# Zeroing a gather table: the whole table, or its border cells alone

## The chip, the cores and the metric

The kernel runs on one core of a Trainium2 chip. The metric is the device time of one launch in microseconds. Five engines matter: PE (TensorE, matmuls), DVE (VectorE), ACT (ScalarE), POOL (GpSimd) and SP (SyncE, which here only issues transfers). Each works through its own list of instructions in order. Transfers between HBM and on-chip memory (SBUF) run on 16 DMA engines that all queues share. In this kernel SP feeds the queue that the profile calls q1 (hardware_dynamic), and POOL feeds q0 (software_dynamic).

## The reference, cut to what matters

The input is an image batch `x` of shape (2, 64, 64, 128). Four layers follow each other, each adding to `x`: layer 0 is a convolution with a selective scan in four directions; layer 1 is a deformable 3x3 convolution; layer 2 is a second scan model and a spectral convolution; layer 3 is a linear attention and a mixture of experts. Each needs the whole output of the one before.

The change is in layer 1. For each output pixel and each of 9 taps a learned offset gives a fractional position; the four pixels around it are gathered, weighted and summed, and a pixel outside the image counts as zero:

```python
def gather(yi, xi):
    valid = (yi >= 0) & (yi < H) & (xi >= 0) & (xi < W)
    yc = jnp.clip(yi, 0, H - 1)
    xc = jnp.clip(xi, 0, W - 1)
    v = x[b_idx, yc, xc]
    return v * valid[..., None].astype(x.dtype)
val = gather(y0i, x0i) * ((1 - wy) * (1 - wx))[..., None] + gather(y0i, x0i + 1) * ((1 - wy) * wx)[..., None] + gather(y0i + 1, x0i) * (wy * (1 - wx))[..., None] + gather(y0i + 1, x0i + 1) * (wy * wx)[..., None]
out = jnp.einsum('bhwkc,kcf->bhwf', val, kernel.reshape(KK, C, F))
```

## The kernel before, in words

**The table.** Layer 1 gathers from a table in HBM. For each image it has 67 x 67 cells (`TS` = 67), and a cell holds the four neighbouring pixels of one position side by side: 4 quadrants of C = 128 floats, 2,048 bytes. Both images make 2 x 67 x 67 x 2,048 bytes = 18.39 MB. Positions are clamped so that every gather lands inside the table (lines 498 to 503), and a quadrant that lies outside the image must read as zero. Layer 1 writes the image into the table with 16 transfers on SP's queue (line 462). Quadrant (dy, dx) is written to rows 2-dy to 65-dy and columns 2-dx to 65-dx. So the cells in rows 2 to 64 and columns 2 to 64 get all four quadrants from the image, and rows and columns 0, 1, 65 and 66 keep zeros in some quadrant or in all.

**Where the zeros come from.** `zero_table` (line 412) runs at the very beginning, before layer 0. It sets a tile `z` of 128 x 536 floats to zero with POOL and sends it over the whole table with one transfer on POOL's queue: 8,576 pieces of 2,144 bytes. The tile is in a pool of its own (`zt`, line 1355) that is given back at once, so that the first tiles of layer 0 lie in the same memory: `w_xp` (line 169), `w_dt`, `sel` (line 174), `w_out`, `mean_w` (line 180), `an` and `dd`. Their first writers have to wait until the zero transfer has read `z` to the end. These writers are SP's loads of `w_xp`, `w_dt` and `w_out`, DVE's memset of `sel`, and ACT's exponential that makes `an` (line 183).

**What goes on at the same time.** SP loads two vectors of parameters (`pv`, `rv`), then the image `X` in eight transfers of 512 KB (`move`, line 1333; layer 0's first image is the first four), then the 64 KB matrix `gmat` (line 200) and `w_in`. [...] Layer 0 then begins with image 0: PE transposes `X` (line 95), DVE gathers statistics (`groupnorm`, line 126: lines 132 to 146), PE averages them over channel groups with `gmat` (lines 136 and 143), DVE makes the inverse root (`rsqrt`, lines 81 to 87) and normalises `xt` (line 146). With that PE computes `pz` (line 209) and `px` (line 221), then the depthwise convolution as 288 matmuls `pc` (line 227). Only then does the scan loop start (lines 241 to 376).

**Order.** The code is written with a tile framework. The list of each engine is ordered when the program is built, by a scheduler that has its own idea of how long a transfer takes, and waits are put in where memory is reused. So instructions that stand at one place in the source can be issued earlier or later than their line says.

Of the kernel before, what the change touches and what calls it, by code (L numbers as in the profile page):

```python
# [16 lines left out]
F32 = mybir.dt.float32  # L17
# [8 lines left out]
P = 128  # L26
B, HH, WW, C = 2, 64, 64, 128
# [13 lines left out]
TS = 67  # L41
# [369 lines left out]

def zero_table(k, pool, table):

    nc = k.nc
    row = B * TS * 4
    z = pool.tile([P, row], F32, name="zero")
    nc.gpsimd.memset(z, 0.0)
    flat = table.rearrange("a c -> (a c)").rearrange("(p g f) -> p g f", p=P, f=row)
    nc.gpsimd.dma_start(out=flat, in_=z.unsqueeze(1).to_broadcast([P, TS, row]))


def layer1(k, table):
# [915 lines left out]
def kernel(tc, ins, out, stages=STAGES):  # L1338
    nc = tc.nc
    with ExitStack() as es:  # L1340
# [8 lines left out]
        if two or "0" in stages or "1" in stages:  # L1349
            with tc.tile_pool(name="x01", bufs=1) as xp:  # L1350
                k.X = xp.tile([P, NT, C], F32, name="X")
                move(nc, k.X, tokens(x))
                if "1" in stages:
                    table = dr.tile([B * TS * TS, 4 * C], F32, name="table")
                    with tc.tile_pool(name="zt", bufs=1) as zp:
                        zero_table(k, zp, table)
                if "0" in stages:
                    layer0(k)
                with ExitStack() as e2:
                    if two:  # L1360
                        mix = mixing_weights(k, dr, e2)
                    if "1" in stages:
                        layer1(k, table)
                    if two:
                        weights = mix()
                if two:
                    norm_tokens(k, rs, sh)
                x = dr.tile([B * L, C], F32, name="x1")
                move(nc, tokens(x), k.X)
# [119 lines left out]
```

## Time and profile before

| | us |
|---|---|
| median of 3 runs | 16227.84 |
| lowest and highest | 16219.87 and 16235.26 |
| the profiled execution, its time | 16221.3 |
| its span, first to last instruction | 16219.5 |
| busy in the span: DVE | 13938.5 |
| POOL | 13438.3 |
| PE | 12269.0 |
| ACT | 9683.1 |

The span is the profiled execution from its first instruction to its last; 1.8 us lie around it. Its time lies 6.5 us below the median of the runs. Busy times of engines overlap and don't add up to the span.

A view by time windows gives, for each stretch, the busy time of each engine with its number of instructions, the TensorE clock that was granted (PEclk, 1.00 is full speed), the busy share of the DMA engines and what they moved. A view of waits says for how long an engine sat idle before a group of instructions and what ended that. A view of transfers gives, by queue, packets, megabytes, and the time that these packets took as a share of 16 engines over the window. The timeline gives start and length in us.

### The profile page before, as it was taken

The numbers are of one execution on the slowest core, as the hardware profiler recorded it, in microseconds if no ns is written. First come the engines' busy times: TensorE is split into PE (matmuls) and PEld (weight loads), VectorE is DVE, ScalarE is ACT, GpSimd is POOL, SyncE is SP. The second block draws the span as 40 slices with busy tenths as digits, with TensorE's granted clock in tenths as the row PEclk, the third lists the DMA queues.
The fourth block names the chain that finished last, engine by engine and source line by source line (L and its number), as shares of the span: only waits on it lengthen the run. The fifth ranks groups of instructions, "written<-read, shape, count | busy, mean of one in ns | idle before, by whom it ended". The sixth has DMA issues, their size and how long they took to land.

```text
span 16219.5 us, 191958 instructions
## 1 busy us (share of the span) xinstructions
PE 12269.0 (76%) x69886; PEld 7241.8 (45%) x69886; DVE 13938.5 (86%) x13011; ACT 9683.1 (60%) x15720; POOL 13438.3 (83%) x4181
## 2 busy tenths in 40 slices
PE   6666657666657874548688688888888888888897
PEld 2222223222225861215455355555545555555565
DVE  4999985999974349999999999999999999999973
ACT  3555534555520017777777677777777777777752
POOL 3888744888735879999999999999999999999970
PEclk8999989999988886769899799999999999999998
DMA  2111111111125544546565555655666666665553
GB/s 101 68 68 66 66 48 52 68 68 66 66 73 162 161 146 151 164 153 198 180 195 193 171 187 192 195 190 196 189 199 195 192 204 196 188 205 195 187 173 128
DMA packets 1214866, 2389.74 MB, mean 147 GB/s; under 512 B 346648, under 2 KB 923288, under 8 KB 1047904
## 3 DMA queue, kind: packets, MB, share of 16 engines
q1 hardware_dynamic: 1162672, 2206.74, 41.5%
q0 software_dynamic: 50384, 169.42, 3.5%
q8 instruction: 552, 9.04, 0.2%
q14 instruction: 394, 3.23, 0.1%
q10 hardware_dynamic: 864, 1.32, 0.0%
HBM read 2018.49 MB, written 358.65 MB: 147 GB/s over the span
## 4 chain that ended last, share of the span: by engine, by line
POOL 39%; DVE 18%; PE 15%; issue 5%; ACT 3%; DMA 3%; another core or an unknown queue 1%; SPq 0%; POOLq 0%; DVEq 0%; ACTq 0%
POOL S L1064 33%; DVE S L1120 11%; PE pef L948 6%; DVE S L347 5%; POOL G L516 2%; PE Z L1082 2%; DMA row<-drow 2%; PE acc L921 2%; POOL S L342 2%; PE pv L535 1%; PE pw L747 1%; PE po L468 1%; POOL S L1070 1%; DVE M L361 1%
## 5 line engine op out<-in xcount | busy, mean ns | idle before, releaser
L1120 DVE TENSOR_TENSOR_SCAN S<-dA,S 128x512 f32<-128x512 f32 x8192 | 9225.0, 1200 | 391.1 <-ACT dA L1118 209.4
L1064 POOL TENSOR_TENSOR S<-row,g 128x4096 f32<-128x4096 f32 x1024 | 9102.1, 8896 | 251.8 <-DMA row<-drow 191.1
L1118 ACT ACTIVATE dA<-row,a_t 128x512 f32<-128x512 f32 x8192 | 5615.4, 692 | 2148.0 <-DVE S L1120 2111.3
L1082 PE MATMUL Z<-S,cv 128*32 128x256 f32 x32768 | 2503.1, 435 | 1481.5 <-ACT ze L1088 1225.6
L948 PE MATMUL pef<-hk,ur 128*128 128x256 f32 x14336 | 3515.4, 388 | 135.4 <-ACT e L928 119.9
L948 PEld LDWEIGHTS pef<-hk,ur 128*128 128x128 f32 x14336 | 2647.1, 191 | 1076.7 <-issue 565.5
L342 POOL TENSOR_TENSOR S<-du,br 128x1024 f32<-128x1024 f32 x1024 | 2389.7, 2355 | 204.8 <-issue 109.2
L347 DVE TENSOR_TENSOR_SCAN S<-dA,stt,S 128x512 f32<-128x512 f32 x1792 | 2198.3, 1268 | 127.7 <-POOL S L342 95.5
L1082 PEld LDWEIGHTS Z<-S,cv 128*32 128x32 f32 x32768 | 1000.8, 121 | 2690.6 <-issue 1283.4
L376 PE MATMUL yp<-M,ident 128*128 128x512 f32 x4096 | 2091.7, 635 | 3.2 <-DVE M L361 3.2
L376 PEld LDWEIGHTS yp<-M,ident 128*128 128x128 f32 x4096 | 821.5, 201 | 2180.2 <-issue 2141.7
L345 ACT ACTIVATE dA<-dt,an 128x512 f32<-128x512 f32 x2048 | 1332.3, 680 | 187.5 <-DVE S L347 173.3
L316 PE MATMUL pcn<-cs,sel 80*128 80x512 bf16 x1024 | 405.6, 396 | 1261.6 <-DVE M L361 1212.4
L361 DVE TENSOR_TENSOR M<-S,pcn 128x1024 f32<-128x1024 f32 x1024 | 1250.6, 1221 | 108.2 <-PE pcn L316 4.8
L1088 ACT COPY ze<-Z 128x512 f32<-128x512 f32 x1024 | 1122.9, 1097 | 234.1 <-PE Z L1082 200.2
L921 PE MATMUL acc<-e,mw 128*128 128x512 f32 x1920 | 1043.5, 631 | 31.7 <-ACT e L928 31.1
L516 POOL DMA_INDIRECT G<-table,idx x576 | 797.1, 1384 | 261.1 <-issue 175.1
L349 ACT COPY stt<-S 128x2 f32<-128x2 f32 x896 | 170.8, 191 | 1376.3 <-DVE S L347 1365.7
L948 PEld LDWEIGHTS pef<-hd,ur 128*128 128x128 f32 x4096 | 758.1, 194 | 493.9 <-issue 235.4
L948 PE MATMUL pef<-hd,ur 128*128 128x256 f32 (+1 forms) x4096 | 876.7, 340 | 103.2 <-ACT e L928 97.2
L523 DVE TENSOR_TENSOR V<-G,wt 128x4608 f32<-128x4608 f32 x64 | 317.6, 4962 | 603.3 <-DMA G<-table,idx 594.8
L279 POOL TENSOR_TENSOR r<-xd,cs 80x512 f32<-80x512 f32 x64 | 73.8, 1152 | 798.2 <-ACT cs L265 798.2
(319 smaller groups left out, 9010.1 us busy)
## 6 DMA issues: line engine op xcount, KB each, us to landing
row<-drow SPq DMA_DIRECT2D x1024, 1024.0 KB
br<-bc SPq DMA_DIRECT2D x256, 1024.0 KB
zd<-ze SPq DMA_DIRECT2D x1024, 256.0 KB
hk<-in_phi_dram SPq DMA_DIRECT2D x128, 576.5 KB
hk<-in_phi_dram SPq DMA_DIRECT2D x96, 704.5 KB
hd<-in_phi_dram SPq DMA_DIRECT2D x512, 128.5 KB
mw<-wdr SPq DMA_DIRECT2D x480, 128.0 KB
hk<-in_phi_dram SPq DMA_DIRECT2D x160, 320.5 KB
```

Of the source, the lines that this page charges most:

```text
L342: nc.gpsimd.tensor_tensor(S, du, br[:, n % 4, :].unsqueeze(1).to_broadcast([P, 2, T]), ALU.mult)
L345: nc.scalar.activation(dA, dt[:, h, :], AF.Exp, scale=an[:, kk * 2 + h, n : n + 1])
L347: nc.vector.tensor_tensor_scan(S[:, h, s_], dA[:, s_], S[:, h, s_], init, ALU.mult, ALU.add)
L361: nc.vector.tensor_tensor(M, S, pcn.unsqueeze(1).to_broadcast([P, 2, T]), ALU.mult)
L376: nc.tensor.matmul(yp[:, h, :], k.ident, M[:, h, :], start=False, stop=n == 15)
L921: nc.tensor.matmul(acc.rearrange("p a s -> p (a s)"), ms[f][:, o, :], e, start=box["first"], stop="whole" in box and (f, o) == todo[-1])
L948: nc.tensor.matmul(pe[:, a, 256 - n :], ur[:, par, j, :], h[:, at : at + n], start=i == 0, stop=i + 1 == len(mm))
L1064: nc.gpsimd.tensor_tensor(S, row.unsqueeze(1).to_broadcast([P, 2, R, T]), g.unsqueeze(2).to_broadcast([P, 2, R, T]), ALU.mult)
L1082: nc.tensor.matmul(Z[32 * j : 32 * j + 32, q], cv[:, h, s], S[:, h, :, s], start=h == 0, stop=h == 1)
L1088: nc.scalar.copy(ze.rearrange("p q t e -> p q e t"), Z)
L1118: nc.scalar.activation(dA, row[:, j % R, :], AF.Exp, scale=a_t[:, h, d : d + 1])
L1120: nc.vector.tensor_tensor_scan(s, dA, s, 0.0, ALU.mult, ALU.add)
```

## The change: what it does

`zero_table` no longer fills the whole table. For each of the two images it sends two transfers of 128 x 536 floats (rows 0 and 1, rows 65 and 66, 274 KB each) and one of 64 x 2,048 floats (524 KB): 64 runs of four cells, each the last two cells of a row and the first two of the next. That is 2.15 MB in six transfers, all on POOL's queue. The tile `z` becomes 128 x 2,048 floats.

```diff
 def zero_table(k, pool, table):
 
+
     nc = k.nc
-    row = B * TS * 4
-    z = pool.tile([P, row], F32, name="zero")
+    z = pool.tile([P, 4 * 4 * C], F32, name="zero")
     nc.gpsimd.memset(z, 0.0)
-    flat = table.rearrange("a c -> (a c)").rearrange("(p g f) -> p g f", p=P, f=row)
-    nc.gpsimd.dma_start(out=flat, in_=z.unsqueeze(1).to_broadcast([P, TS, row]))
+    flat = table.rearrange("a c -> (a c)")
+    cell = 4 * C
+    for b in range(B):
+        at = b * TS * TS * cell
+
+        for y in (0, TS - 2):
+            rows = flat[at + y * TS * cell : at + (y + 2) * TS * cell].rearrange("(p f) -> p f", p=P)
+            nc.gpsimd.dma_start(out=rows, in_=z[:, : 2 * TS * cell // P])
+
+        edge = flat[at + (TS + TS - 2) * cell :]
+        dst = bass.AP(edge.tensor, edge.offset, [[TS * cell, TS - 3], [1, 4 * cell]])
+        nc.gpsimd.dma_start(out=dst, in_=z[: TS - 3, :])
```

The built program differs from the one before in more than these lines, all of it in the first stage of layer 0. Line numbers are those of the kernel before; `+` and `-` show where rows stand in the list of an engine (PE's list is the same):

```diff
 DVE
  L84  gn_s<-gn_rs
+ L175 memset sel          (waits for the six zero transfers)
+ L181 memset mean_w
+ L177 sel<-ident x3
+ L184 an<-an              (waits for ACT)
+ L187 dd<-ident,pv x8
  L85  gn_s<-gn_s,gn_v
  L86, L87, L146 xt<-xt,gn_mg,gn_rs, then four copies xp<-px
- L175, L181, L177 x3, L184, L187 x8, the same rows
 ACT
  L82  sqrt gn_s<-gn_v
+ L183 table load (waits for the six zero transfers), exp an<-pv
  L211 table load, then silu z<-pz and copies xp<-px
- L183 table load, exp an<-pv
- L228 table load
 SP
  L200 gmat, L202 w_in
+ L170 w_xp (waits for the six zero transfers), L172 w_dt, L179 w_out
  L212 zs<-z x16
- L170 w_xp, L172 w_dt, L179 w_out
 POOL
- L419 table<-zero, 8576 pieces
+ L425 table<-zero 128x536 x4
  L151 to L154 memsets xp, L151 memset xp
+ L429 table<-zero 64x2048 (waits for the two row transfers of image 0)
+ L429 table<-zero 64x2048 (waits for those of image 1)
  L152 to L154 memsets xp
```

The numbers 425 and 429 are lines of the changed kernel. From the scan loop of layer 0 on every engine issues the same instructions in the same order; only which of eight semaphores a transfer on POOL's queue counts on is shifted.

## The prediction

> **What bounds the kernel now.** I read the page's head first, for the span that every sum below is made against:
>
> ```profile
> span 16219.5 us, 191958 instructions
> ```
>
> The chain that ended last is mostly scan work of layers 2 and 0, which the change doesn't touch. The zeros go out in the first microseconds, so I cut the start into windows (columns: window and length, busy time with instruction count by engine, PEclk, DMA share, GB/s):
>
> ```profile
> 0.00:62.00 62.00, 7.57 (x32) 6.28 (x32) 13.30 (x28) 4.91 (x6) 5.24 (x16) 0.62 0.98 374
> 62.00:69.00 7.00, 1.50 (x5) 1.42 (x6) 4.52 (x15) 1.49 (x2) 0.00 (x0) 0.50 0.01 2
> 69.00:92.00 23.00, 23.00 (x49) 9.94 (x49) 2.95 (x5) 11.39 (x20) 0.00 (x0) 0.91 0.59 212
> 92.00:206.00 114.00, 114.00 (x267) 50.26 (x266) 8.97 (x18) 14.57 (x21) 0.00 (x0) 1.00 0.00 1
> ```
>
> The engines nearly idle for 62 us while the DMA engines are full (0.98); DVE then works through the normalisation for 7 us; PE is busy without a gap to 206 us, and the scan loop comes after that. The start is one serial chain: whatever ends its first stretch sooner moves everything behind it. PE's waits in 0 to 210 us say what ends it:
>
> ```profile
> PE pt L95 <- DMA X<-in_x_dram: 29.1, 3, 11.1
> PE pm L136 <- DMA gmat<-in_gmat_dram: 25.7, 1, 25.7
> ```
>
> PE waits for pieces of X and last for gmat, which stands behind all of X in SP's queue; pm starts at 62.41 us. What fills the DMA engines is the view of transfers, 12 to 55 us:
>
> ```profile
> q0 software_dynamic: 3704, 15.88, 89.4%
> q1 hardware_dynamic: 3702, 1.87, 14.4%
> ```
>
> The zeros on q0 take nine tenths of the engines, and X on q1 gets one packet for each of theirs (3702 to 3704). So zeros move at 15.88 MB / (43 us x 0.894) = 413 GB/s of engine time. Both queues over 0 to 64 us, then q1 over 0 to 6 us, and over 4.5 to 6 us, where X has the engines alone:
>
> ```profile
> q0 software_dynamic: 4304, 18.39, 69.5%
> q1 hardware_dynamic: 8896, 4.83, 25.5%
> ```
> ```profile
> q1 hardware_dynamic: 1467, 0.90, 56.4%
> ```
> ```profile
> DMA packets 892, 0.46 MB, mean 306 GB/s; under 512 B 12, under 2 KB 892, under 8 KB 892
> ```
>
> gmat is in after 4.83 - 0.26 (w_in, behind it) = 4.57 MB of q1. The sum 6.0 + (4.57 - 0.90)/306 GB/s + 18.39/413 GB/s = 6.0 + 12.0 + 44.5 = 62.5 us reproduces the 62.4 of the trace, so I use the same sum for the changed kernel.
>
> [...] equal packet counts above, though a packet of zeros is 4288 B and one of X 512 B. [...] No row here shows a 64-row transfer from POOL. [...] (PEclk 0.50 from 62 to 69 us), and this will be so again.
>
> **The change part by part.**
>
> *Fewer zeros.* 18.39 - 2.15 = 16.24 MB less at 413 GB/s: -39.3 us. All six transfers fall before X ends, so all 2.15 MB still delay gmat, by 5.2 us. gmat lands at 6.0 + 12.0 + 5.2 = 23.2 us. The statistics must be ready too: the last piece of X for image 0 reached PE at 34.77 us and gn_mv ended at 40.61, 5.8 us later. Half of X (2.10 MB, with 0.31 MB of vectors ahead, 0.90 MB in by 6.0) is in at 6.0 + 1.51/306 + at most 5.2 = 16.1 us, so gn_mv ends by 22 us, just under gmat. gmat still sets the time; were the zeros out of X's way altogether, gn_mv would cap the further gain at about 1.5 us.
>
> *DVE's block in the chain.* sel, mean_w, an and dd now stand between L84 and L85, inside the inverse root that xt waits for. Today they run beside 62 us of convolution on PE:
>
> ```profile
> 91.81 0.91 DVE L175 MEMSET sel<- 80x1024 uint32 x1 [0.16 <-issue]
> 92.70 0.17 DVE L181 MEMSET mean_w<- 128x128 f32 x1
> 92.79 3.65 DVE L177 CAST sel<-ident 16x2048 bf16<-16x2048 f32 x3
> 96.45 0.23 DVE L184 TENSOR_SCALAR an<-an 128x128 f32<-128x128 f32 x1
> 96.59 1.65 DVE L187 TENSOR_SCALAR dd<-ident,pv 128x128 f32<-128x128 f32 x8
> ```
>
> From 91.81 to 98.24: 6.4 us. In the new place nothing covers it: PE waits for xt, ACT for pz. +6.4 us. PE has no gap from 68.6 to 206 us, so leaving the old place gives nothing back.
>
> *Waits of that block.* sel waits for all six zero transfers; queued behind it on DVE are L85 to L146, and behind those PE. The row transfers need one POOL issue each. The nearest row is the gather (128 pieces, L516): 0.95 us of issue, one per 1.25 us. So four are issued by about 7 us. The first zeros packets flow near 6 us in the old kernel (q1 alone until then). [...] Rows land by 12 us, the edges, which wait for them, by 18 us. The block starts at 23.2 + 3 = 26 us: 8 us of cover, and the wait costs nothing. Each microsecond of landing after 26 costs one.
>
> *ACT.* Two table loads of 1.28 us and the exponential of 0.31 us now stand ahead of the first z: 2.9 us, beside the 6.4 us of DVE and the 2.4 us of xt, so nothing; an is ready 1.6 us after the square root, before DVE's casts end. The removed third load (1.28 us) lay beside PE's convolution and gives nothing.
>
> *SP and POOL.* Three loads move ahead of the 16 stores of z; they are issued at about 25 us in some 1.2 us, and the first store isn't due before 38 us. POOL stands before its last three memsets until the rows land; the convolution reads them near 60 us. The larger memset of z is 128x2048 against 128x536 at 0.55 us: some 2 us on POOL, before the row transfers, inside the cover. From the scan loop on nothing changes in order, so the saving at 206 us should reach the end.
>
> *Sum.* -39.3 + 6.4 = **-32.9 us**. Profiled execution: 16221.3 to 16188.4. The median of the runs stands 6.5 us above it; I apply the saving there: **16195 us**.
>
> **The rivals.**
>
> *Same or slower through a late wait (slower).* The wait of DVE's sel on the zero transfers takes the place of gmat's. It decides once the last of them lands after 26 us, and the kernel gets slower once it lands after 26 + 33 = 59 us, which is where the full 18 MB end today. That would take all six transfers on one DMA engine: 2.15 MB at 413/16 = 26 GB/s is 83 us, landing at about 88, so 16228 + 29 = 16257 us. [...] 4%.
>
> *Partly eaten.* The two edges alone on one engine each: 0.52 MB / 26 GB/s = 20 us, which delays that engine's share of X and so gmat by up to 18 us: 16228 - 15 = 16213. Or X alone doesn't keep 306 GB/s: at 240 GB/s the 3.67 MB take 15.3 instead of 12.0 us, 16198. 10%.
>
> *The block is covered.* If gmat or the statistics came so that DVE's block cost nothing, the whole 39 us would show: 16189. The order of one engine's list speaks against it: L85 can't pass it. 7%.
>
> *No change at the end.* A later stage takes up the gain, for instance the scan loop falling into another rhythm: 16228. Layers wait for each other and nothing outside this chain has a clock of its own; 4%.
>
> **How the numbers follow.** My forecast has 75%, with its own range of 16183 to 16207: 2 us each way on the sum (the statistics' cap below, X's rate and half-clock matmuls above) and up to 10 us for the median of a few runs, since three runs lay within 15 us. About 0.2% of the time, 32.5 us, is what a measurement of this kernel can tell from no change. My -32.9 falls on that line, so the forecast gives slightly more than half of its chance to faster: 0.41, and 0.34 to within. With the covered block, faster is 0.48; within is 0.34 + 0.10 + 0.04 = 0.48; slower 0.04. The range for all cases, 8 in 10, is 16181 to 16210, towards the partly eaten case.
>
> **What would show it.** PE's pm starts near 23 us instead of 62.4, with gmat as its releaser; q0 carries 2.15 MB; DVE's sel memset starts about 26 us without a wait; xt starts some 6.4 us later after L84 than today; PE's pz starts near 36 us (68.6 today) and the first pd near 191 us (223.6 today); q0's share in the first 25 us is about 5 us. The prediction is wrong if pm waits for statistics or a late X, if sel shows an idle wait for a transfer into the table, or if the 33 us at the first pd are not there at the end.

## The result and the profile after

| | before | after |
|---|---|---|
| median of 22 runs each, us | 16231.93 | 16200.64 |
| lowest and highest, us | 16216.26 and 16240.26 | 16187.30 and 16222.14 |
| span of the profiled execution, us | 16219.5 | 16192.2 |

The ratio is 0.9982, with a 95% interval of 0.9975 to 0.9988: 31.3 us or 0.19% faster. A gain is clear, but it lies just inside the 0.2% that the prediction named as the limit for one measurement.

The start in windows (columns as before: window and length, busy time with instruction count for PE, PEld, DVE, ACT and POOL, then PEclk, DMA share, GB/s):

```profile
0.00:24.00 24.00, 6.49 (x32) 5.51 (x32) 10.64 (x28) 4.91 (x6) 7.01 (x21) 0.82 0.93 291
24.00:36.00 12.00, 1.11 (x4) 1.00 (x4) 9.70 (x29) 3.08 (x4) 0.00 (x0) 0.50 0.17 57
36.00:60.00 24.00, 22.79 (x47) 10.06 (x48) 3.19 (x4) 11.21 (x19) 0.00 (x0) 0.86 0.47 176
60.00:174.00 114.00, 114.00 (x267) 50.11 (x266) 3.46 (x5) 11.88 (x18) 0.00 (x0) 1.00 0.00 0
```

The first stretch, in which the DMA engines are full (0.93) and the others wait, has shrunk from 62 to 24 us. The second, in which DVE works alone and PE's clock reads 0.50, has grown from 7 to 12 us: DVE's busy time there is 9.70 us, against 4.52 us before. After that PE is busy without a gap, as it was.

The chain's marks in the timeline of PE (start, length; in brackets PE's idle time before it and what ended that), before:

```profile
62.41 0.56 PE L136 MATMUL pm<-gn_mv,gmat 128*128 128x1 f32 x2 [25.70 <-DMA gmat<-in_gmat_dram]
...
68.61 16.31 PE L209 MATMUL pz<-xt,w_in 128*128 128x512 f32 x32 [3.95 <-issue]
...
223.64 1.98 PE L257 MATMUL pd<-uc,w_xp 128*128 128x512 f32 x4 [1.37 <-ACT uc L253]
```

and after:

```profile
24.36 0.56 PE L136 MATMUL pm<-gn_mv,gmat 128*128 128x1 f32 x2 [7.25 <-DMA gmat<-in_gmat_dram]
...
37.21 16.79 PE L209 MATMUL pz<-xt,w_in 128*128 128x512 f32 x32 [10.61 <-issue]
...
192.72 1.98 PE L257 MATMUL pd<-uc,w_xp 128*128 128x512 f32 x4 [1.37 <-ACT uc L253]
```

So pm is 38.05 us sooner, pz 31.40 us, and the first pd of the scan loop 30.92 us. gmat still releases pm, after 7.25 us of waiting in place of 25.70; SP issues it behind its last piece of X, at 19.58 us in place of 55.73. The difference between the first two gains is DVE's block: pz - pm grew from 6.20 to 12.85 us. The wait before pz, put down to "issue", is DVE's part of the chain, 10.61 us in place of 3.95. It grew because of what stands in DVE's list. The timeline of DVE (start, length), before:

```profile
65.33 0.16 DVE L84 TENSOR_TENSOR gn_s<-gn_rs 128x1 f32<-128x1 f32 x1
65.52 0.16 DVE L85 TENSOR_TENSOR gn_s<-gn_s,gn_v 128x1 f32<-128x1 f32 x1
```

and after, cut to four rows:

```profile
27.27 0.16 DVE L84 TENSOR_TENSOR gn_s<-gn_rs 128x1 f32<-128x1 f32 x1
27.78 0.91 DVE L175 MEMSET sel<- 80x1024 uint32 x1 [0.35 <-issue]
...
32.56 1.65 DVE L187 TENSOR_SCALAR dd<-ident,pv 128x128 f32<-128x128 f32 x8
34.13 0.15 DVE L85 TENSOR_TENSOR gn_s<-gn_s,gn_v 128x1 f32<-128x1 f32 x1
```

L85 starts 6.86 us after L84; before it was 0.19 us. Its operands were there (gn_v since 26.80 us, gn_s since 27.43), but it stands behind the block in DVE's list. So the block of sel, mean_w, an and dd costs 6.67 us here. In front of sel DVE idles for 0.35 us, and no transfer is named: the zeros were in long before. The transfers of 0 to 30 us show them (packets, MB, share of 16 engines over the window):

```profile
q1 hardware_dynamic: 9456, 5.52, 61.5%
q0 software_dynamic: 480, 2.15, 19.5%
```

All 2.15 MB are there. They took 0.195 x 30 = 5.85 us of the engines' time. In 18 to 30 us the same view has only 0.02 MB left on q0, and none of it after 19 us, so the last of them landed about 9 us before sel.

The medians carry these 31 us to the end. The two profiled executions alone differ by 27.3 us of span, but one execution can't tell 4 us at the end: the stage of layer 2, from the first to the last `S<-row,g` of POOL, took 9675.8 us in the profile of before, 9679.6 us in that of after, and from 9675.4 to 9693.4 us over all the profiles of this study. I therefore read early marks from profiles and the end from medians.

### The profile page after: what moved, and what is told of

Its sections match the earlier page's. It is cut to its first block, busy times and chain, and to the rows that moved or that the text cites. A ratio compares the mean times of both kernels' runs of the same rounds, so it can differ in the third digit from the quotient of the medians.

```text
span 16192.2 us, 191978 instructions
## 1 busy us (share of the span) xinstructions
PE 12275.8 (76%) x69886; PEld 7241.7 (45%) x69886; DVE 13933.9 (86%) x13011; ACT 9680.3 (60%) x15719; POOL 13438.6 (83%) x4186
## 4 chain that ended last, share of the span: by engine, by line
POOL 39%; DVE 18%; PE 14%; issue 6%; ACT 3%; DMA 3%; SPq 0%; POOLq 0%; another core or an unknown queue 0%; DVEq 0%; ACTq 0%
POOL S L1074 32%; DVE S L1130 11%; PE pef L958 6%; DVE S L347 5%; POOL G L526 3%; PE Z L1092 2%; PE acc L931 2%; POOL S L342 2%; DMA row<-drow 2%; PE pw L757 1%; PE po L478 1%; POOL S L1080 1%; ACT dA L1128 1%; DVE M L361 1%; POOL u L294 1%
```

## The experiments

My theory had two terms: every megabyte of zeros ahead of gmat delays the chain by 1/413 GB/s, or 2.4 us, and DVE's block costs 6.4 us because it now stands in the chain. The main rivals were that the block is covered or would cost the same elsewhere, that removing zeros isn't worth time in proportion, and that the gain at the scan loop is lost later. In the short diffs `zero_table` and the pools are abridged. All kernels of this section compute the whole result. The comparisons of a set were made on one chip with common runs of the kernel before.

### Block early, with border zeros (e1)

The tile `z` keeps its own memory as long as layer 0 lasts, so that the first tiles of layer 0 don't lie in it and have nothing to wait for. `z` has 536 floats again, and an edge is sent as four repeats of 512 floats.

```diff
-    z = pool.tile([P, 4 * 4 * C], F32, name="zero")
+    z = pool.tile([P, B * TS * 4], F32, name="zero")
...
-        nc.gpsimd.dma_start(out=dst, in_=z[: TS - 3, :])
+        nc.gpsimd.dma_start(out=dst, in_=z[: TS - 3, :cell].unsqueeze(1).to_broadcast([TS - 3, 4, cell]))
...
-                    with tc.tile_pool(name="zt", bufs=1) as zp:
-                        zero_table(k, zp, table)
-                if "0" in stages:
+                with tc.tile_pool(name="zt", bufs=1) as zp:
+                    zero_table(k, zp, table)
                     layer0(k)
```

> Border zeros as in the changed kernel, but the zero tile has memory of its own while layer 0 runs, so DVE's block (sel, mean_w, an, dd) stands at the very start of DVE's list and waits for no transfer; three loads (0.67 MB) stand ahead of gmat. My theory (the block cost the changed kernel 6.7 us between L84 and L85; gmat is bound by bytes ahead of it): pm at 24.4 + 0.67/306 = 26.6 us, pz 6.2 us after pm (12.9 in the changed kernel), so 32.8 us, first pd at 188.3, and about 35 us below the kernel before. Rival (the block costs nothing where it stands): pz stays 12.9 us after pm, near 39.5 us, pd near 195, and 29 us below the kernel before.

Measured: 16199.25 against 16234.92 us, ratio 0.998 (0.9971 to 0.9988), -35.7 us. The timeline of DVE:

```profile
1.15 0.91 DVE L175 MEMSET sel<- 80x1024 uint32 x1 [0.16 <-issue]
...
29.10 0.16 DVE L81 TENSOR_SCALAR gn_v<-pq 128x1 f32<-128x1 f32 x1 [0.28 <-PE pq L143]
29.18 1.84 DVE L215 TENSOR_SCALAR dw<-ident,pv 128x128 f32<-128x128 f32 x9
30.94 0.15 DVE L83 RECIPROCAL gn_rs<-gn_s 128x1 f32<-128x1 f32 x1
```

and that of PE:

```profile
26.88 0.56 PE L136 MATMUL pm<-gn_mv,gmat 128*128 128x1 f32 x2 [9.59 <-DMA gmat<-in_gmat_dram]
...
34.47 16.97 PE L209 MATMUL pz<-xt,w_in 128*128 128x512 f32 x32 [5.41 <-issue]
```

sel is done at 2 us, while DVE would wait for X. pz - pm falls from 12.85 to 7.59 us: 5.26 us of the block's 6.67 are won. The other 1.4 us went to something I had not thought of. With the block gone to the front, nine of the little products `dw` (L215), which DVE used to do during the wait for X, now stand between L81 and L83: 1.84 us from start to start, where the kernel before took 0.43 (64.70 to 65.13). The scheduler filled the hole with other work. So the block's cost is real, but moving it to the front doesn't give all of it back. pm itself comes 2.5 us later than in the changed kernel (26.88 for 24.36), since the loads of w_xp, w_dt and w_out, 0.67 MB, now stand ahead of gmat; 2.5 us of gain are left at pd.

### Block early, with all 18 MB of zeros (e5)

Only the last part of e1's edit, on the kernel before.

```diff
-                    with tc.tile_pool(name="zt", bufs=1) as zp:
-                        zero_table(k, zp, table)
-                if "0" in stages:
+                with tc.tile_pool(name="zt", bufs=1) as zp:
+                    zero_table(k, zp, table)
                     layer0(k)
```

> The kernel before with all its 18.39 MB of zeros from the start, and one thing changed: the zero tile has memory of its own while layer 0 runs, so DVE's block stands at the start and 0.67 MB of loads stand ahead of gmat. My theory (the wait for the reused memory cost the kernel before nothing; the zeros beside X did): pm at 62.4 + 0.67/306 = 64.6 us, pz 7.6 us after it as in the run with the border and the block early, so 72.2 us, pd near 227.5, and 0 to 5 us above the kernel before. Rival (what the change freed is the wait for the tile's memory, not the DMA engines): as fast as the changed kernel, about 30 us below.

Measured: 16234.43 against 16233.04 us, ratio 1.0001 (0.9993 to 1.0009). In the timeline of PE pm still waits for gmat behind the zeros:

```profile
65.09 0.56 PE L136 MATMUL pm<-gn_mv,gmat 128*128 128x1 f32 x2 [27.38 <-DMA gmat<-in_gmat_dram]
```

Freeing the block of its wait shows no gain by itself: pd starts 3.3 us later than before. In the kernel before the block was covered by the convolution, so there was nothing to win, and the 1.4 us of `dw` come on top (pz - pm 7.59 us). At the start of the kernel the gain of the change comes from the bytes ahead of gmat alone.

### Half of the zeros removed (e2, e7)

The changed kernel, but image 0's table is filled whole and only image 1's has the border alone: 10.27 MB in five transfers.

```diff
     for b in range(B):
         at = b * TS * TS * cell
+        if b == 0:
+            row = B * TS * 4
+            bulk = flat[: P * 33 * row].rearrange("(p g f) -> p g f", p=P, f=row)
+            nc.gpsimd.dma_start(out=bulk, in_=z[:, :row].unsqueeze(1).to_broadcast([P, 33, row]))
+            last = flat[P * 33 * row : TS * TS * cell].rearrange("(p f) -> p f", p=P)
+            nc.gpsimd.dma_start(out=last, in_=z[:, : row // 2])
+            continue
```

> Table 0 is filled whole, table 1 at its border only: 10.27 MB of zeros, halfway between 18.39 and 2.15, all from the start; DVE's block stands where it stood in the kernel before. My theory (zeros ahead of gmat cost their bytes at 413 GB/s): pm at 62.4 - 8.12/0.413 = 42.7 us, pz at 48.9, pd at 204, some 20 us below the kernel before. Rival (a threshold: once the fill is short enough to end before X, the first stretch doesn't depend on it): pm near 24 to 30 us. Rival (the gain lies elsewhere, in what the scheduler reordered): no change in pm.

> The kernel with half of the zeros once more: at pd it was 18 us ahead of the kernel before, at the end 10. If the 8 us were chance of one chip and session: pd at 205.6 again and 14 to 22 us below at the end. If they are lost in a later stage for a reason that this kernel carries with it: 10 us or less below at the end, and the loss in the same stage of its profile (3 us between pd and layer 0's second image, 3 us in the gathers, the rest in layer 2).

Measured: e2 16225.27 against 16234.92 us, ratio 0.9993 (0.9985 to 1.0002), -9.7 us; e7, the same kernel on another chip, 16223.74 against 16233.04 us, ratio 0.9996 (0.9987 to 1.0004), -9.3 us. The timeline of PE in e2:

```profile
43.84 0.56 PE L136 MATMUL pm<-gn_mv,gmat 128*128 128x1 f32 x2 [6.58 <-DMA gmat<-in_gmat_dram]
```

At the chain's head the proportion holds: 8.12 MB less make pm 18.6 us sooner (e7: 43.47, 18.9 us), where 8.12 / 413 GB/s is 19.7 us. The block stays behind the convolution's input in this kernel (sel at 72.03 us), so pz - pm is 6.2 us as before, and pd starts 18.1 us sooner (e7: 19.2). But by the medians only half of that is there at the end, twice, though each interval still takes in the whole. This pair supports my account of the start and speaks against its last step, "the saving reaches the end". The stages in which the expectation of e7 looked for the loss don't repeat it: layer 2 took 9689.7 us in the profile of e2 and 9682.0 in that of e7.

### Where the half kernel's gain goes: the number of transfers (e8 to e12)

Beside their bytes, these kernels differ in how many transfers of zeros go ahead of the others on POOL's queue, and with that in which of eight semaphores each later one counts on. I tested this number, called "count" in the expectations. e8 cuts the half kernel's large transfer in three:

```diff
-            nc.gpsimd.dma_start(out=bulk, in_=z[:, :row].unsqueeze(1).to_broadcast([P, 33, row]))
+            for g in range(0, 33, 11):
+                nc.gpsimd.dma_start(out=bulk[:, g : g + 11], in_=z[:, :row].unsqueeze(1).to_broadcast([P, 11, row]))
```

e9 cuts the one transfer of the kernel before in four:

```diff
-    nc.gpsimd.dma_start(out=flat, in_=z.unsqueeze(1).to_broadcast([P, TS, row]))
+    for g in range(0, TS, 17):
+        n = min(17, TS - g)
+        nc.gpsimd.dma_start(out=flat[:, g : g + n], in_=z.unsqueeze(1).to_broadcast([P, n, row]))
```

> The half kernel again, its large transfer (33 groups) cut into three of 11 groups, so that six transfers of zeros are issued as in the changed kernel, and not four. The bytes stay 10.27 MB. In all theories gmat ends near 43.5 us, pd starts near 204 to 206 us, about 18 to 19 us sooner than before. Theory 'count': the 9 us that the half kernel lost after pd come from which of the eight semaphores the later transfers on POOL's queue count on, which four transfers shift by another amount than six; then the whole 18 to 19 us arrive at the end, near 16215. Theory 'not the count': the loss has another cause and the end stays 9 us sooner than before, near 16224.

> The kernel before, its one transfer of 18.39 MB cut into four (17, 17, 17 and 16 groups), so that as many transfers are issued as in the half kernel. In all theories gmat ends as before, 62 to 65 us, and pd starts at 223 to 227 us. Theory 'count': the shift by four costs 9 us after pd here too, so the end is about 9 us later than before, near 16242. Theory 'not the count': the end is within 3 us of before, near 16233.

These two texts miscount: the half kernel issues five transfers, not four, so e8 issues seven, and e9 one fewer than the half kernel. Measured: e8 16222.36 against 16234.85 us, ratio 0.9993 (0.9985 to 1.0001), -12.5 us; e9 16238.20 against 16234.85 us, ratio 1.0002 (0.9994 to 1.0011), +3.4 us. Both lie between the two values set down, and because of the miscount they don't decide. e10 is the half kernel with its large transfer cut in two, six in all; e11 is the kernel before with its transfer cut in five; e12 is the changed kernel with two neighbouring row transfers joined, five in all.

```diff
-            nc.gpsimd.dma_start(out=bulk, in_=z[:, :row].unsqueeze(1).to_broadcast([P, 33, row]))
+            for g, n in ((0, 17), (17, 16)):
+                nc.gpsimd.dma_start(out=bulk[:, g : g + n], in_=z[:, :row].unsqueeze(1).to_broadcast([P, n, row]))
```

```diff
-    nc.gpsimd.dma_start(out=flat, in_=z.unsqueeze(1).to_broadcast([P, TS, row]))
+    for g in range(0, TS, 14):
+        n = min(14, TS - g)
+        nc.gpsimd.dma_start(out=flat[:, g : g + n], in_=z.unsqueeze(1).to_broadcast([P, n, row]))
```

```diff
-        for y in (0, TS - 2):
-            rows = flat[at + y * TS * cell : at + (y + 2) * TS * cell].rearrange("(p f) -> p f", p=P)
-            nc.gpsimd.dma_start(out=rows, in_=z[:, : 2 * TS * cell // P])
+        for y, n in ((0, 2), (TS - 2, 4)) if b == 0 else ((TS - 2, 2),):
+            rows = flat[at + y * TS * cell : at + (y + n) * TS * cell].rearrange("(p f) -> p f", p=P)
+            nc.gpsimd.dma_start(out=rows, in_=z[:, : n * TS * cell // P])
```

> The half kernel (e2) issues five transfers of zeros, not four as the expectations of e8 and e9 say, so e8 issued seven and e9 one fewer than the half kernel. Here its large transfer is cut in two (17 and 16 groups), which makes six, as in the changed kernel. pm near 44 us and pd near 204 to 206 us in all theories. Theory 'count' (which of eight semaphores the later transfers on POOL's queue count on causes the loss after pd): the shift is that of the changed kernel, which lost nothing, so the full 18 to 19 us arrive, near 16216. Theory 'not the count': 9 to 13 us sooner than before, as in e2, e7 and e8, near 16223.

> The kernel before, its transfer of 18.39 MB cut into five (four of 14 groups, one of 11), the half kernel's number. pm at 62 to 65 us, pd at 223 to 227 us in all theories. Theory 'count': about 9 us later at the end than before, near 16243. Theory 'not the count': within 3 us of what pd loses, 16234 to 16238, as in e9.

> The changed kernel with five transfers of zeros in place of six: rows 65 and 66 of image 0 and rows 0 and 1 of image 1 lie side by side and go out as one transfer of 128 x 1072 floats. The bytes and their place are the same. In all theories pm starts near 24 to 26 us and pd near 192 to 194 us, some 30 us sooner than in the kernel before. Theory 'count' (the later transfers on POOL's queue count on other semaphores when five are issued ahead of them, which cost the half kernels and the kernel before with five transfers 7 to 10 us after pd): the end is only 20 to 24 us sooner than before, near 16210. Theory 'not the count' (the spread of comparisons): 29 to 31 us sooner, near 16202.

Measured: e10 16213.00 against 16232.04 us, ratio 0.9987 (0.9980 to 0.9994), -19.0 us; e11 16239.77 against 16232.04 us, ratio 1.0003 (0.9995 to 1.0012), +7.7 us; e12 16207.10 against 16238.97 us, ratio 0.9981 (0.9973 to 0.9989), -31.9 us. So by the medians the half kernel with six transfers brings the whole gain of its pd to the end, and the kernel before with five loses time although nothing else is changed; the interval of e11 still takes in no change.

e12 did one thing that no theory had set down. The timeline of its DVE:

```profile
28.30 0.16 DVE L84 TENSOR_TENSOR gn_s<-gn_rs 128x1 f32<-128x1 f32 x1
28.49 0.16 DVE L85 TENSOR_TENSOR gn_s<-gn_s,gn_v 128x1 f32<-128x1 f32 x1
...
31.64 0.91 DVE L175 MEMSET sel<- 80x1024 uint32 x1 [0.15 <-issue]
```

With one transfer fewer the scheduler placed the block after xt, beside PE's pz, instead of between L84 and L85. pz - pm is 6.20 us, and pd starts at 187.12 us, 5.6 us sooner than in the changed kernel with pm 1.0 us later. This is the cleanest measurement of the block: moved out of the chain with nothing put in its place, it gives back its 6.65 us whole. At the end 4.6 us of the 36.5 us are missing.

Over all profiles, the loss between pd and the end goes with one stretch: layer 3's loop over experts, from the first `ph` to the last. Two windows over that loop, of the changed kernel and then of e7:

```profile
16085.00:16164.00 79.00, 58.22 (x663) 35.94 (x656) 8.38 (x18) 8.69 (x19) 1.83 (x3) 0.85 0.82 336
```

```profile
16106.00:16192.00 86.00, 66.45 (x661) 41.34 (x661) 8.38 (x18) 8.70 (x19) 1.89 (x3) 0.76 0.74 308
```

DVE, ACT and POOL are busy for as long as before, PE for 8.2 us longer, and the granted clock is 0.76 in place of 0.85. PE's largest group of matmuls by count, in the same windows (busy us, mean ns):

```profile
L1311 PE MATMUL pout<-w,hz 128*32 128x128 f32 x384 | 11.7, 274 | 0.0
```

```profile
L1319 PE MATMUL pout<-w,hz 128*32 128x128 f32 x384 | 16.5, 344 | 0.0
```

It is the same 384 matmuls at 344 ns in place of 274. Within the loop the granted clock of the kernel before and of the changed one is 1.00 or 0.50, in stretches of whole multiples of 3.41 us (the last section shows it). All kernels in one table (sooner than before by pd in the profile and by the median at the end, us; loop: first to last `ph`, us; half: steps of 3.41 us of the loop at clock 0.50, for the other kernels worked out from the mean clock of windows of 10 and 14 us):

| kernel | transfers ahead | pd sooner | end sooner | lost | loop | half |
|---|---|---|---|---|---|---|
| before | 1 | | | | 76.9 | 8 |
| e3 | 1 | 39.8 | 39.5 | 0.3 | 77.4 | 8 |
| e5 | 1 | -3.3 | -1.4 | -1.9 | 77.2 | 8 |
| after | 6 | 30.9 | 31.3 | -0.4 | 77.1 | 7 |
| e6 | 6 | 30.2 | 29.0 | 1.2 | 77.1 | 7 |
| e1 | 6 | 33.5 | 35.7 | -2.2 | 77.0 | 7 |
| e10 | 6 | 18.8 | 19.0 | -0.2 | 77.0 | 7 |
| e4 | 6 | 41.2 | 44.0 | -2.8 | 80.8 | 10 |
| e9 | 4 | -0.7 | -3.4 | 2.7 | 84.1 | 12 |
| e2 | 5 | 18.1 | 9.7 | 8.4 | 82.5 | 11 |
| e7 | 5 | 19.2 | 9.3 | 9.9 | 84.1 | 12 |
| e11 | 5 | -0.5 | -7.7 | 7.2 | 82.5 | 11 |
| e12 | 5 | 36.5 | 31.9 | 4.6 | 84.3 | 12 |
| e8 | 7 | 17.5 | 12.5 | 5.0 | 84.1 | 12 |

The kernels with one or six transfers lose at most 1.2 us; those with four, five or seven lose 2.7 to 9.9, on average 6.3 us, and their loop is 5.5 to 7.3 us longer than 77.0, on average 6.6. The loop's length follows the half-clock steps: 7 or 8 go with 77 us, 10 with 80.8 (e4), 11 with 82.5 and 12 with 84. The averages agree, so on average the loss fits PE at half clock for more of that loop; kernel by kernel the two differ by up to 4.4 us.

That the number of transfers decides it is supported by e10, e11 and the table, but not proved. Each single loss lies within the interval of its comparison (about 13 us to either side), the profiles are one execution each, and e4 has six transfers and a loop of 80.8 us. The loop is not all that varies, either: the profiled execution of e10 was 16.4 us above its median with a loop of 77.0 us, and its layer 2 was the longest of all (9693.4 us). From the first pd on each engine's list is the same in these kernels, apart from which semaphores stand for POOL's transfers and what the first gather waits for. No run changes the semaphores without the number. How a count at the start can reach a clock 16 ms later stays open.

### All the zeros, but late (e3)

The kernel before, with `z` kept over layer 0 and the whole fill of 18.39 MB issued when the first tile of the convolution's output is there. Then the zeros run beside a stretch in which the DMA engines have nothing to do (share 0.00 from 92 to 206 us in the kernel before).

```diff
 def zero_table(k, pool, table):
-    nc = k.nc
-    row = B * TS * 4
-    z = pool.tile([P, row], F32, name="zero")
-    nc.gpsimd.memset(z, 0.0)
...
+    k.z = pool.tile([P, B * TS * 4], F32, name="zero")
+    k.table = table
+
+def late_zero(k, src):
+    nc, table, z = k.nc, k.table, k.z
+    nc.gpsimd.tensor_scalar(z, src, 0.0, None, ALU.mult)
...
                         nc.scalar.activation(U[:, h, q * N : (q + 1) * N], pc, AF.Silu, bias=k.v("conv_b")[:, h : h + 1])
+                    if b == 0 and h == 0:
+                        late_zero(k, U[:, 0, : B * TS * 4])
```

> All 18.39 MB of zeros, but issued when the first half of the convolution's output U is there, in the middle of PE's convolution; the tile is U times 0 and has memory of its own; DVE's block at the start; 0.67 MB ahead of gmat. My theory (not the bytes but their place beside X cost the time): pm at 24.4 + 2.2 - 5.2 = 21.4 us, pz 27.6, pd 183, about 40 us below the kernel before although as many bytes are written, and PE's convolution as long as before (62 us). Rival (18 MB of writes cost wherever they are): within 10 us of the kernel before, with idle time on PE or at pd.

Measured: 16195.43 against 16234.92 us, ratio 0.9976 (0.9967 to 0.9986), -39.5 us. The timeline of PE, and a window over PE's stretch without a gap:

```profile
20.66 0.56 PE L136 MATMUL pm<-gn_mv,gmat 128*128 128x1 f32 x2 [6.40 <-DMA gmat<-in_gmat_dram]
```

```profile
51.00:166.00 115.00, 115.00 (x270) 50.61 (x269) 3.47 (x5) 11.88 (x18) 4.71 (x2) 1.00 0.42 160
```

The zeros are issued at 70.11 us, and PE is busy for all 115 us of the window while the DMA engines move them (share 0.42). pm is at 20.66 us with no zeros ahead of gmat, and pd at 183.82 us, 39.8 us sooner than before; 39.5 us arrive at the end. All 18.39 MB are written, and yet this kernel's median gain is larger than that of the changed one. The two intervals overlap, so the cleanest pair is e3 with e5: in both the block is early and all bytes are written, and only the place of the zeros differs. pm starts at 20.66 us in e3 and at 65.09 in e5, and the medians stand 39.5 us below and 1.4 us above their kernels before. What the kernel before paid for was not the bytes but when they moved.

### Border zeros late, and half of X out of the way (e4)

e3 with the changed kernel's six transfers, and the four transfers of X that belong to image 1 issued after gmat and w_in, right behind w_in's load in layer 0 (`NTB` tokens are one image).

```diff
-                move(nc, k.X, tokens(x))
+                move(nc, k.X, tokens(x), 0, NTB)
+                k.x = x
...
+                if b == 0:
+                    move(nc, X, tokens(k.x), NTB, NT)
...
+                    if b == 0 and h == 0:
+                        late_zero(k, U[:, 0, : B * TS * 4])
```

> Border zeros only, issued late as in the run with all zeros late; DVE's block at the start; the second image's half of X is loaded after gmat and w_in. My theory (with zeros and half of X out of the way the statistics bind pm): gmat lands near 13.5 us, gn_mv ends near 17 us, pm at 17.3, pz 23.5, pd 179, some 44 to 45 us below the kernel before. Rival (X of the first image needs about the 24 us whatever stands behind it): pm stays near 24 us and the time is like that of the changed kernel less the block, 36 us below.

Measured: 16190.88 against 16234.92 us, ratio 0.9974 (0.9964 to 0.9985), -44.0 us. PE's waits over the first 180 us:

```profile
PE pm L136 <- DVE gn_mv L133: 5.6, 1, 5.6
```

Now pm waits for the statistics and no longer for gmat: it starts at 19.35 us (17.3 had been expected), pd at 182.49 us. That is 1.3 us sooner than in e3. With the zeros and the second image gone from the front, gn_mv (18.88 us) comes last, so the statistics do put a cap on this step. The two kernels' intervals overlap, so only the marks tell e4 from e3. Its median is the lowest of all the kernels here: 44.0 us below its kernel before, where the changed kernel is 31.3 and 29.0 us below.

### The changed kernel again (e6)

The edit is that of the change; the comparison was made on another chip.

> The changed kernel itself, beside the others on one chip. My theory: pm 24.4, pz 37.2, pd 192.7 us as in its profile, and 31 us below the kernel before at the end. Rival (some of the 31 us at pd is given back later): pd the same, 20 us or less below at the end.

Measured: 16204.08 against 16233.04 us, ratio 0.9981 (0.9974 to 0.9987), -29.0 us. In its profile pm starts at 26.18 us, again released by gmat. It came 1.8 us later than in the first profile of the same kernel, pz - pm is 12.85 us again, and pd starts at 193.49 us. The gain repeats, within 2.3 us.

### The chain's head against the bytes in front of it

| zeros moved ahead of gmat | kernels | pm starts at, us |
|---|---|---|
| 18.39 MB | before, e11, e9, e5 | 62.41, 63.28, 63.46, 65.09 |
| 10.27 MB | e7, e2, e10, e8 | 43.47, 43.84, 43.93, 44.61 |
| 2.15 MB | after, e12, e6, e1 | 24.36, 25.38, 26.18, 26.88 |
| none | e3, e4 | 20.66, 19.35 |

From before to after the slope is 38.05 us / 16.24 MB = 2.34 us per MB, from before to e3 41.75 / 18.39 = 2.27. The prediction's 1/413 GB/s is 2.42. Different sizes and shapes of the zeros fall on one line to within about 3 us. Part of the spread is known: in e1, e3 and e5 the 0.67 MB of w_xp, w_dt and w_out stand ahead of gmat too, by the prediction's 306 GB/s an estimated 2.2 us. e4 is no point of this line, since gmat doesn't release its pm.

## Why the prediction was right

*Fewer zeros, -39.3 us.* Right in kind, 1.3 us too large: pm moved by 38.05 us, to 24.36 in place of 23.2 (26.18 in e6). Two terms of the sum make up most of the difference. The 2.15 MB took 5.85 us of the engines' time where 5.2 were set, and X with the other loads ran at 5.52 MB / (0.615 x 30 us) = 299 GB/s where 306 were set. In e6 that rate is 5.52 MB / (0.657 x 30 us) = 280 GB/s, and by 6.0 us q1 had moved 0.66 MB (0.84 in the first profile, 0.90 in the sum), in line with its later pm.

*gn_mv under gmat.* Right: it ended at 20.65 + 0.37 = 21.0 us, where at most 22 were set, and gmat was the releaser. The cap on a further gain was wrong in size. The prediction put 1.5 us on taking the zeros out of X's way altogether; e3 did that, and its pm came 3.7 us sooner with gmat still the releaser. The step that failed is that gn_mv was left at 22 us, a figure that holds the same 5.2 us of zeros. The statistics came last only in e4, with half of X out of the way as well, 5.0 us below the changed kernel's pm.

*DVE's block in the chain, +6.4 us.* Right: 6.67 us between L84 and L85, and 6.65 us more from pm to pz. The rival "the block is covered" falls on this row, and e1 and e5 show both sides of it: away from the chain it gives 5.3 us back in e1 and the whole 6.65 in e12, and in the kernel before it had cost nothing.

*Waits of that block.* The result was right, the way to it wasn't. sel waited for no transfer. But both bounds for the zeros, an estimate of mine that no view of the kernel before showed, were missed. The rows were to land by 12 us: POOL could go on to the first edge, behind the rows of image 0, at 11.57 us, and to the second, behind those of image 1, at 13.07 us (13.28 and 14.78 us in e6). The changed kernel shows more than 8 us from the first issue at 3.00 us to landing beside X; q0's first packets appear between 6 and 7 us, so 3 to 4 us pass before anything moves at all. The edges were to land by 18 us: q0's last packets fall between 18 and 19 us, in e6 between 20 and 22. The term stayed at nothing because the cover was wide: sel started at 27.78 us (29.60 in e6), more than 7 us after the last packet. The slower rival, a late wait on few DMA engines, needed a landing after 59 us; it didn't occur (the 5.85 us of 16 engines would be an estimated 94 us on a single one, and q0's packets all fell between 6 and 19 us). A kernel that forces it was not tried.

*ACT, SP and POOL at nothing.* No wait for any of them shows up in the chain. ACT's two table loads lie at 27.12 to 30.02 us, beside DVE's block, and POOL's larger memset of `z` took 1.81 us (some 2 were set).

*pz, pd and the end.* pz at 37.21 (36 set), pd at 192.72 (191 set), late by 1.2 and 1.7 us, of which pm's delay is 1.2. The 30.9 us at pd (30.2 in e6) became 31.3 and 29.0 us at the end. "The saving reaches the end" held for the changed kernel. It was less sure than written: the prediction said that nothing outside this chain has a clock of its own, and in the kernels with four, five or seven transfers 3 to 10 us were lost again after pd, along with more half-clock steps of PE in layer 3 (supported by the table, not proved). With one row transfer fewer the change is in that group (e12), though its earlier pd made up for it there.

*The time.* 16200.64 against 16195: 5.6 us above. Of these 4.1 us are the kernel before, whose median was 16227.84 over three runs and 16231.93 over 22; 1.6 us are the sum (-31.3 for -32.9). The forecast sat on the 0.2% line, and the result ended just inside it.

## What to carry to other kernels

In these runs the background fill was paid by what shared the DMA engines with it. Look at which load stands last in the opening chain and what moves beside it, and before making a fill smaller see whether it can move under a stretch where those engines idle (e3 wrote all 18.39 MB under PE's convolution, at a DMA share of 0.42, and gained 39.5 us). Releasing memory sooner lets a scheduler issue the next tiles' writers sooner, and that can put them into a serial chain; compare each engine's order before and after, and price what lands in the chain by its own duration (6.7 us here, beside 38 us won at pm). Loads that the chain needs soon, however small, go ahead of bulk that it needs late (e4 did it with half of X and all the zeros, and its pm came 5.0 us sooner than the changed kernel's; gmat ahead of all of X was not tried).

## What the runs showed of the hardware that was not expected

PE's granted clock in one loop 16 ms after the edit differs from kernel to kernel (0.85 against 0.76 on average over the loop) though the loop's lists are the same, and the same matmul (`pout`, 128x128 out) takes 274 or 344 ns on average with it. Over 10 us the clock can read as a value between half and full: in e7 the stretch of 16159 to 16169 us has 0.84, where the same stretch of the changed kernel (16138 to 16148) has 1.00. Cut finer, it is an average of the two. Two windows of e7, 52.0 us and 55.4 us into the loop:

```profile
16158.00:16161.40 3.40, 3.40 (x57) 3.18 (x60) 0.22 (x1) 0.26 (x1) 0.00 (x0) 0.50 1.03 443
16161.40:16164.80 3.40, 2.90 (x34) 1.21 (x26) 0.00 (x0) 0.92 (x2) 0.00 (x0) 1.00 0.98 414
```

And the window of the changed kernel 52.0 us into its loop:

```profile
16136.70:16140.10 3.40, 2.94 (x72) 2.65 (x72) 0.23 (x1) 0.60 (x3) 0.00 (x0) 1.00 1.04 448
```

In windows of 0.1 us, over the first 80 us and over the loop, the clock of the kernel before and of the changed one reads 0.50 or 1.00 in all windows but those in which it changes. Before, it is 0.50 from 15.29 to 73.32 us, and in the loop for 20.48, 3.41 and 3.41 us; in the changed kernel from 15.58 to 42.89 us, and in the loop for 23.89 us. These are 17, 6, 1 and 1 steps of 3.41 us, and 8 and 7. In the other twelve kernels the time at half clock over 94 us from the loop's start, worked out from windows of 10 and 14 us, comes to 8 to 13 such steps, within 0.1 of a whole number. What tips a step to half clock here is not shown: in the 10 us from 43 us into the loop on PE was busy for 8.66 us in e7 and for 8.43 us in the changed kernel, and only e7's clock fell (0.95 against 1.00).

The same kernel's first loads ran at 299 and at 280 GB/s in two profiled executions.
